# One level of Strassen's scheme for three adjacency products, with quarter sums kept in DRAM and layer 1 split into three runs of stages

## The chip, the cores and the metric

The kernel runs on one core of a Trainium2 chip. The metric is device time in microseconds (us), lower is better. Five engines take part, each with its own in-order stream of instructions: TensorE (PE in the profile, with its weight loads PEld), VectorE (DVE), ScalarE (ACT), GpSimd (POOL) and SyncE (SP). POOL, SP and ACT also issue DMA transfers. Whatever an engine has to wait for holds up everything behind it in its own stream.

## The reference

Two graph layers follow one another on x of shape (8, 2048, 64): 8 batches, 2048 nodes, 64 features. Everything is float32. Cut to what matters:

```python
# layer 0: supports I, A, 2AA - I     layer 1: supports I, A, 2AA - I, softmax(relu(E E^T))
w   = einsum('nd,dkio->nkio', embedding, weight)   # a weight matrix per node and support
x_g = einsum('knm,bmc->bnkc', supports, x)         # each support applied to x
out = einsum('bnki,nkio->bno', x_g, w) + embedding @ bias
x   = layernorm(x + out)
```

A is the 2048x2048 adjacency. With all batches side by side x is a 2048x512 matrix. Nobody forms AA: u = A x is computed first and then v = A u, so each layer has two products of the 2048x2048 matrix with a 2048x512 one. Layer 1 has a third one with the softmax matrix, s x.

## The kernel before

**Tiling.** Nodes are cut into 8 blocks of 256 (two slabs of 128 rows). A stage makes one block of one product. There are 32 stages in a row: stages 0 to 7 make u of layer 0, 8 to 15 make v of layer 0, 16 to 23 make u of layer 1, and 24 to 31 make v of layer 1 followed by z = s x for the same block. The adjacency streams in from DRAM through four tiles `a` of 512 KB, each holding four 128-row steps of the sum for a block, loaded by SP in the order of use (class `Ahead`). x and u stay in SBUF as 16 slabs of 128x512 each.

**Two ways to multiply.** For u, `product_u` holds a 128x128 piece of A still and moves a slab of x past it, 512 columns at a time: 32 matmuls a stage, output rows are nodes (`pu`). For v and z, `turned` holds a 128x128 piece of u or x still and moves 256 columns of A or of the softmax: 64 matmuls a stage and product, with features in the output's rows (`pv`). A float32 matmul leaves two records in the trace; the matmuls of `weights` use a faster number format and leave one.

**What rides beside a product.** The weights per node are made by `weights(g)`: two matmuls `pw` into a PSUM pair (`ps_big`, two pairs, shared by everything but the products) and one copy into `w_room`, by VectorE for even g and ScalarE for odd g; 16 g a stage, 8 for v of layer 0. `turn` transposes u or x so that features lie in the rows of `t` (8 transposes and 4 copies). `apply(c)` multiplies features with weights in small matmuls `po` and adds the result into `acc` on VectorE (operation SCALAR_TENSOR_TENSOR); four c a stage. `post` normalises the block on VectorE and ScalarE in three parts and stores it. In layer 0's v stages `scores_of_rows` and `statistics` also find the maximum and the sum of each softmax row: a maximum on VectorE, relu and exp on ScalarE, and then a reciprocal on VectorE that waits for the exp. The `scores` of z make the softmax tiles `p`.

**What sets the order.** The order is written by hand. Every job has a stage and a place from 0 to 64 within it (to 128 in the last eight stages), the function `put(n, place, f)`. The main loop runs the product of stage n, counts places (2 for a matmul of 512 columns, 1 for one of 256), and emits each job when its place is reached. `Pinned` keeps program order on each engine. Most of a stage's own finishing work (`weights`, `turn`, `apply`, `post`) is put into the following stage. In the last eight stages the weights share the stage's 128 places with two products.

**Ends.** A u stage ends with `end_u`, which copies PSUM into the slabs of `u_all`, one slab on VectorE and one on ScalarE. A v stage ends with `end_v`: in layer 0 this is put at place 6 of the next stage, and its result is needed by `apply` at place 20.

Of the kernel before, what the change touches and what calls it, by code (L numbers as in the profile page):

```python
# [8 lines left out]
F32 = mybir.dt.float32  # L9
# [5 lines left out]
P = 128  # L15
# [32 lines left out]
def two_graph_layers(ctx: ExitStack, tc: tile.TileContext, x, x_t, adj_b, layers, out):  # L48
# [30 lines left out]
    ps_acc = ctx.enter_context(tc.tile_pool(name="ps_acc", bufs=2, space=PSUM))  # L79
# [17 lines left out]
    X = [None] * NJ  # L97
# [3 lines left out]
    def new_x(j):  # L101
        X[j] = feat.tile([P, BC], F32, tag=f"x{j}", name=f"x{j}")
        return X[j]

    for j in range(NJ):
        act.dma_start(out=new_x(j), in_=x[j * P:(j + 1) * P, :])
# [75 lines left out]
    x1d = [dram.tile([NB * B, C], F32, tag=f"x1d{j}", name=f"x1d{j}") for j in range(NBLK)]  # L182
    cd = [dram.tile([2, SB, P], F32, tag=f"cd{j}", name=f"cd{j}") for j in range(NBLK)]
# [4 lines left out]
    def load_s1():  # L188
        for q in range(4):
            pool.dma_start(out=s1[q * D:(q + 1) * D, :].bitcast(F32), in_=estk[1][(q // 2) * D:(q // 2 + 1) * D, :])  # L190

    class Ahead:
# [6 lines left out]
        def next(self):  # L199
            while (len(self.ready) < self.bufs and self.order  # L200
# [6 lines left out]
    adj = Ahead(4, lambda: stream.tile([P, 4, NB], F32, tag="a", name="a"),  # L207
                lambda t, jm: sp.dma_start(out=t, in_=adj_b[jm[0]][:, jm[1]:jm[1] + 4, :]),
                [(j, m) for _ in range(4) for j in range(NBLK) for m in range(0, NJ, 4)])
# [5 lines left out]
    class Stage:  # L215
        def __init__(self, n, li, kk, j):
            self.n, self.li, self.kk, self.j = n, li, kk, j
            self.half = (li, kk) == (0, 1)
            self.units = C // 2 if self.half else C
            self.e01 = e01[n % 2]  # L220
            self.t = None


        def load_e(self):
# [5 lines left out]
            if (self.li, self.kk) == (1, 1):  # L230
                self.c = two.tile([P, 2, NB], F32, tag="c", name="c")
                pool.dma_start(out=self.c, in_=cd[self.j].rearrange("k s p -> k (s p)").partition_broadcast(P))
# [71 lines left out]
        def post(self, part, s0=0, s1=GROUPS):  # L304
# [20 lines left out]
            else:  # L325
# [10 lines left out]
                for s in range(s0 * SB // GROUPS, s1 * SB // GROUPS):  # L336
                    queue.dma_start(out=new_x(SB * self.j + s), in_=nodes[s * P:(s + 1) * P, :])


        def turn(self, k, slabs):  # L340
            ps = big("pt")
            psv = ps.rearrange("p a (q n) -> p (a q) n", n=P)
            for s in range(SB):
                for q in range(BQ):
                    pe.transpose(psv[:, s * BQ + q, :], slabs[SB * self.j + s][:, q * P:(q + 1) * P], ident)
            t = self.features()
            for s in range(SB):
                for par in range(2):
                    src = psv[64 * par:64 * par + 64, s * BQ:(s + 1) * BQ, :]
                    copy(s, t[64 * k:64 * k + 64, s * P:(s + 1) * P, par::2], src.rearrange("p q n -> p n q"))  # L350


        def graph(self):
            if self.kk == 0:
                return [(self.product_u(), self.end_u)]
            v = (self.turned(U, self.adjacency()), self.end_v)
            return [v] if self.li == 0 else [v, (self.turned(X, self.softmax()), self.end_z)]

        def adjacency(self):
            a = None  # L360
            for m in range(NJ):
                if m % 4 == 0:
                    a = adj.next()
                yield a[:, m % 4, :]
# [5 lines left out]
        def product_u(self):  # L370
            self.acc_u = ps_acc.tile([P, SB, BC], F32, tag="acc", name="pu")
            for m, a in enumerate(self.adjacency()):
                for s in range(SB):
                    pe.matmul(self.acc_u[:, s, :], a[:, s * P:(s + 1) * P], X[m],
                              start=(m == 0), stop=(m == NJ - 1))
                    yield 2

        def end_u(self):
            for s in range(SB):
                j = SB * self.j + s  # L380
                copy(s, U[j], self.acc_u[:, s, :])

        def turned(self, stationary, moving):


            self.acc_t = ps_acc.tile([P, BQ, NB], F32, tag="acc", name="pv")
            for m, a in enumerate(moving):
                for q in range(BQ):
                    pe.matmul(self.acc_t[:, q, :], stationary[m][:, q * P:(q + 1) * P], a,
                              start=(m == 0 and q % 2 == 0), stop=(m == NJ - 1 and q % 2 == 1))  # L390
                    yield 1

        def end_v(self):
            t = self.features()
            for h in range(2 if self.half else 1):
                for par in range(2):
                    src = self.acc_t[64 * par:64 * par + 64, :, :].rearrange("p q n -> p n q")
                    copy(1 - h, t[64 * h:64 * h + 64, :, par::2], src, 2.0)

        def end_z(self):  # L400
            t = self.features()
            for half in range(SB):
                n = slice(half * P, half * P + P)
                for par in range(2):
                    r = slice(64 * par, 64 * par + 64)
                    dve.tensor_tensor(t[64:128, n, par::2], self.acc_t[r, :, n].rearrange("p q n -> p n q"),
                                      self.c[r, 1, n, None].to_broadcast([64, P, BQ]), op=ALU.mult)
# [16 lines left out]
        def scores_of_rows(self, s, h):  # L424
# [9 lines left out]
            act.activation(w_room[:, (s + 4) * N + h * 1024:(s + 4) * N + (h + 1) * 1024], flat, AF.Relu)  # L434

        def statistics(self, s):
            j = SB * self.j + s
            r = w_room[:, (s + 4) * N:(s + 5) * N]
# [13 lines left out]


    later = [(0, 1, c) for c in range(V1 // 8)] + [(1, k, c) for k in range(2) for c in range(V0 // 8)]
    stages = [Stage(n, n // 16, n // 8 % 2, n % 8) for n in range(32)]
    stages[0].load_e()
    def units(x):
        return x.rearrange("p j x -> p (j x)").rearrange("p (v x) -> p v x", v=8)

    for c in range(V0 // 8):  # L460
        load_weights(0, 0, c, (units(u_all[:, 4 + 3 * c:6 + 3 * c, :]), units(u_all[:, 6 + 3 * c:7 + 3 * c, :])))
    split_rooms = [one.tile([P, 8, P], F32R, tag="wsplit", name="wsplit"),
                   one.tile([P, 8, P], F32R, tag="wraw", name="wsplit"),
                   units(u_all[:, 2:4, :]).bitcast(F32R),
                   one.tile([P, 8, P], F32R, tag="sq", name="wsplit")]
    for c in range(2):
        wst.ready.append(split_weights(0, 0, c, split_rooms[c]))
    wst.order = wst.order[2:]
    plans = [{} for _ in stages]

    def put(n, i, f, *args):
        plans[n].setdefault(i, []).append((f, args))

    def spread(n, first, last, jobs):
        for i, job in enumerate(jobs):
            put(n, first + (last - first) * i // max(len(jobs) - 1, 1), *job)

    for n, st in enumerate(stages):
        late = n < 24
        weights = [(st.weights, g) for g in range(st.units // 4)]  # L480
        if n == 15:
            spread(n, 44, 62, weights)
        elif st.half:
            spread(n + 1, 2, 16, weights)
        elif late:
            spread(n + 1, 1, 34, weights)
        else:
            spread(n, 52 if n == 24 else 28, 124, weights)
        if n + 1 < len(stages):
            if st.kk == 0:  # L490
                put(n + 1, 37, st.turn, 1, U)
            at, gap, posts = (8, 11, None) if n == 15 else (20, 14, 44) if st.half else (42, 9, 56) if late else (10, 9, 24)
            for c in range(4):
                put(n + 1, at + gap * (c // 2), st.apply, c)
            if n == 15:
                for k in range(6):
                    put(n + 1, (17 if k < 3 else 29) + k, st.post, k % 3, k // 3 * 8, k // 3 * 8 + 8)
            else:
                for k in range(3):
                    put(n + 1, posts + (3 if late else 4) * k, st.post, k)  # L500
# [96 lines left out]
```

## Time and profile before

| | before |
|---|---|
| median of 3 runs | 1678.39 us |
| lowest, highest of the 3 | 1666.79, 1689.35 us |
| the profiled execution | 1671.0 us |
| its span on the core | 1669.2 us |
| PE, PEld busy | 1609.2, 1117.6 us |
| DVE, ACT, POOL busy | 852.2, 469.0, 161.3 us |
| DMA moved | 206.38 MB, mean 124 GB/s |
| PE instructions | 10528 |

The span is the time from the first to the last instruction of one execution; the profiled execution's own time stands beside it. Busy times of the engines overlap one another. The profile also gives the clock granted to TensorE (PEclk, 1.00 is full speed); over the span its mean was 0.991.

The stages can be found in the trace by their ends (the copies `u<-pu` and `t<-pv`). Layer 0's u stages run from the start to 353.5 us, its v stages to 703.6 us, layer 1's u stages to 1061.4 us, and its v and z stages to 1649.5 us. The rest is the last block's finish.

### The profile page before, as it was taken

To read this page: it belongs to the slowest core of one execution; us is meant where nothing else is said; L and a number is where in the kernel's file an instruction comes from. 1 tells how busy PE (TensorE), PEld (TensorE's weight loads), DVE (VectorE), ACT (ScalarE), POOL (GpSimd) and SP (SyncE) were. 2 spreads that over 40 slices of the span, in tenths; PEclk is the share of its full clock that TensorE was granted. 3 is DMA by queue.
4 is the path that set the end of the run, shared out by engine and by line. 5 is a ranking of instruction groups with operands and counts; after the bars stand their busy time and mean duration, and the time that the engine had idled before them with its cause. 6 is when DMAs were issued, how large, how long until landed. Compare 5 with 4: busy or idle time off the path is not lost.

```text
span 1669.2 us, 24536 instructions
## 1 busy us (share of the span) xinstructions
PE 1609.2 (96%) x10528; PEld 1117.6 (67%) x10528; DVE 852.2 (51%) x1348; ACT 469.0 (28%) x518; POOL 161.3 (10%) x263
## 2 busy tenths in 40 slices
PE   8899999999899999899999999999999999999996
PEld 3455555567777777654555555778888888888885
DVE  3545555556676566664544444444353534425345
ACT  0122222222344444431222222231322314132231
POOL 4111111100111111110000000000000000000000
PEclk9999999999999999999999999999999999999998
DMA  9555665553545554445444444422231313223100
GB/s 353 180 167 171 188 192 175 187 164 120 144 133 137 112 116 118 110 100 136 128 142 142 130 141 137 141 85 73 89 98 48 101 60 95 66 77 98 51 26 13
DMA packets 63979, 206.38 MB, mean 124 GB/s; under 512 B 13056, under 2 KB 13056, under 8 KB 63296
## 3 DMA queue, kind: packets, MB, share of 16 engines
q1 hardware_dynamic: 38752, 126.37, 26.1%
q0 software_dynamic: 19648, 64.82, 13.3%
q10 hardware_dynamic: 5472, 13.63, 2.3%
q8 instruction: 83, 1.36, 0.3%
q14 instruction: 24, 0.20, 0.0%
HBM read 171.19 MB, written 33.57 MB: 123 GB/s over the span
## 4 chain that ended last, share of the span: by engine, by line
PE 53%; DVE 3%; issue 1%; DMA 1%; ACT 1%; SPq 0%; ACTq 0%
PE pv L42 26%; PE pu L42 11%; PE pw L42 7%; PE po L42 6%; DVE acc L42 1%; PE ps L42 1%; DMA wst<-wd 1%; PE pt L42 1%; DVE w L42 1%; ACT w L42 0%; ACT t L42 0%; DVE mean L42 0%; DVE dev L42 0%; DVE top L42 0%; DVE t L42 0%
## 5 line engine op out<-in xcount | busy, mean ns | idle before, releaser
L42 PE MATMUL pu<-x,a 128*128 128x512 f32 x1024 | 493.5, 600 | 5.8 <-DMA x<-in_x 5.8
L42 PE MATMUL pv<-a,u 128*128 128x256 f32 x2048 | 488.1, 384 | 7.4 <-issue 7.3
L42 DVE COPY w<-pw 128x1024 f32<-128x1024 f32 x224 | 273.8, 1224 | 323.2 <-PE pw L42 322.6
L42 PEld LDWEIGHTS pv<-a,u 128*128 128x128 f32 x2048 | 387.3, 191 | 75.9 <-issue 20.2
L42 PE MATMUL pw<-e,wst 128*128 128x512 f32 x880 | 394.9, 530 | 17.7 <-DMA wst<-wd 8.8
L42 ACT ACTIVATE w<-pw 128x1024 f32<-128x1024 f32 x224 | 229.1, 1023 | 421.8 <-PE pw L42 419.9
L42 DVE SCALAR_TENSOR_TENSOR acc<-po,mask,acc 128x256 f32<-128x256 f32 (+1 forms) x640 | 249.4, 427 | 179.6 <-PE po L42 157.4
L42 PEld LDWEIGHTS pu<-x,a 128*128 128x128 f32 x1024 | 190.1, 191 | 146.0 <-issue 120.7
L42 PEld LDWEIGHTS pw<-e,wst 128*128 128x128 f32 x880 | 164.3, 191 | 147.0 <-issue 94.1
L42 PE MATMUL pv<-p,x 128*128 128x256 f32 x1024 | 239.7, 379 | 0.0
L42 PE MATMUL po<-w,t 128*32 128x256 f32 (+1 forms) x5120 | 210.5, 338 | 6.1 <-issue 3.0
L42 PEld LDWEIGHTS pv<-p,x 128*128 128x128 f32 x1024 | 191.6, 190 | 26.6
L42 PEld LDWEIGHTS po<-w,t 128*32 128x32 f32 (+1 forms) x5120 | 124.8, 108 | 98.9 <-issue 39.8
L42 DVE SCALAR_TENSOR_TENSOR p<-ps,c 128x512 f32<-128x512 f32 x64 | 44.1, 689 | 92.9 <-PE ps L42 92.8
L42 ACT ACTIVATE p<-p 128x512 f32<-128x512 f32 x64 | 40.3, 630 | 117.3 <-DVE p L42 117.1
L42 ACT ACTIVATE sq<-acc 128x1024 f32<-128x1024 f32 (+2 forms) x20 | 17.7, 886 | 188.9 <-DVE acc L42 179.2
L42 ACT ACTIVATE w<-pr 128x1024 f32<-128x1024 f32 x32 | 32.7, 1023 | 116.2 <-DVE top L42 115.5
L42 ACT ACTIVATE u<-pu 128x512 f32<-128x512 f32 x16 | 9.6, 597 | 188.7 <-DVE u L42 188.7
L42 POOL DMA_DIRECT2D e<-ed x64 | 33.6, 530 | 288.8 <-PE pw L42 287.4
L42 DVE COPY t<-pt 64x512 f32<-64x512 f32 x48 | 33.1, 689 | 53.5 <-PE pt L42 50.4
L42 ACT ACTIVATE t<-pt 64x512 f32<-64x512 f32 x48 | 31.3, 651 | 103.3 <-DVE t L42 103.1
L42 ACT ACT_TABLE_LOAD x30 | 38.5, 1283 | 53.4 <-DVE p L42 27.4
(73 smaller groups left out, 632.0 us busy)
## 6 DMA issues: line engine op xcount, KB each, us to landing
a<-in_adj_b SPq DMA_DIRECT2D x128, 512.0 KB, 4.2
wst<-wd SPq DMA_DIRECT2D x110, 512.0 KB, 4.5
bx<-bx POOLq DMA_DIRECT2D x32, 256.0 KB, 3.0
acc<-bx POOLq DMA_DIRECT2D x16, 512.0 KB, 5.7
pd<-acc POOLq DMA_DIRECT2D x16, 512.0 KB, 2.9
acc<-pd POOLq DMA_DIRECT2D x16, 512.0 KB, 5.7
wd<-wsplit POOLq DMA_DIRECT2D x13, 512.0 KB
wraw<-in_w ACTq DMA_DIRECT2D x10, 512.0 KB, 7.9
```

Source lines behind the costliest of these rows:

```text
L42: return self._tc.keep_in_program_order(f(*args, **kwargs))
```

## The change

Stages are now named by a letter and a layer: A0 (u of layer 0), B0 (v of layer 0), A1 (u of layer 1), Z1 (z) and V1 (v of layer 1), eight each, 40 in all. Layer 1's v and z no longer share a stage: all of A1 comes first, then all of Z1, then all of V1; z goes to DRAM (`zd`) and comes back (`load_z`) for the V1 stage of its block.

**Strassen.** For B0, A1 and V1, blocks 1 to 7 are made from seven products of quarter size in place of eight (`strassen`). A block of A has 2x2 quarters (two slabs of rows, even and odd 128-column pieces); the right matrix has 2x2 quarters too (even and odd slabs, left and right 256 columns). Seven times eight matmuls of 256 columns are issued: 56 of the places, so `length` is 56 and every place is scaled by 56/64. VectorE forms the four results from the seven products with seven additions of 256 columns; ScalarE copies two of the products. Block 0 of each run stays `plain` (32 matmuls of 512 columns, all in the form that holds A still), and so do all of A0 and Z1.

**Sums of A.** While A0 reads the adjacency, `sums_of_a` makes the four sums of quarters on VectorE, four operations for each of the four `a` tiles of a stage, into one buffer `r`, which POOL stores in DRAM (`sd`). Later stages read three plain quarters and four sums: seven tiles of 512 KB a stage.

**Sums of the right matrix.** T1 to T4 are made once a phase by `Sums.make`, in operations of 2048 columns: during stage 8 (and the start of stage 9) for B0, during stage 16 for A1, and during stage 32 (and the start of 33) for V1. They lie in unused parts of `w_room`, in `u_all` and in `x_all`. As A1's sums overwrite u's place, A1's results go to a small tile `v` and to DRAM (`ud`), and SP reads them back in the Z1 stages.

**Turns.** As v now comes out with nodes in its rows, it must be transposed: `turn` runs for B0 and V1 also, at place 4 (B0) or 3 (V1) of the next stage. It is 8 transposes, with 8 copies in B0 and 4 in V1. `end_v` is gone. The accumulators in PSUM are four single banks in place of two pairs.

The core of the diff; `put(9, 0, ...)` is emitted before the first matmul of the stage:

```diff
-    ps_acc = ctx.enter_context(tc.tile_pool(name="ps_acc", bufs=2, space=PSUM))
+    ps_acc = ctx.enter_context(tc.tile_pool(name="ps_acc", bufs=4, space=PSUM))
...
+    plain = {("A0", j) for j in range(NBLK)} | {(phase, 0) for phase in ("B0", "A1", "V1")}
...
+    lefts = [("quarter", (0, 0)), ("quarter", (0, 1)), ("quarter", (1, 1)),
+             ("sum", 1), ("sum", 0), ("sum", 2), ("sum", 3)]
...
+        def turn(self, k, feature=None):
+            slabs = X[SB * self.j:SB * self.j + SB] if feature == "x" else self.slabs
+            scale = 2.0 if self.kk else None
...
             for s in range(SB):
-                for par in range(2):
-                    src = psv[64 * par:64 * par + 64, s * BQ:(s + 1) * BQ, :]
-                    copy(s, t[64 * k:64 * k + 64, s * P:(s + 1) * P, par::2], src.rearrange("p q n -> p n q"))
+                for h in range(2 if self.half else 1):
+                    for par in range(2):
+                        src = psv[64 * par:64 * par + 64, s * BQ:(s + 1) * BQ, :]
+                        copy(s, t[64 * (k + h):64 * (k + h) + 64, s * P:(s + 1) * P, par::2],
+                             src.rearrange("p q n -> p n q"), scale)
...
+        def strassen(self, right):
...
+            def times(name, what):
+                made[name] = acc = self.accumulator(name)[:, 0:half]
+                a = adj.next().rearrange("p (k n) -> p k n", n=P)
+                for k in range(k_slab):
+                    pe.matmul(acc, a[:, k, :], rights[what](k), start=(k == 0), stop=(k == k_slab - 1))
+                    yield 1
+            yield from times("p1", "B11")
+            act.copy(p1, made["p1"])
+            yield from times("p2", "B21")
+            add(c11, made["p2"], p1)
+            yield from times("p4", "T4")
+            act.copy(p4, made["p4"])
+            yield from times("p6", "T2")
+            add(u2, made["p6"], p1)
+            yield from times("p5", "T1")
+            add(u4, made["p5"], u2)
+            yield from times("p7", "T3")
+            add(c21, made["p7"], u2)
+            add(c22, made["p5"], c21)
+            add(c21, c21, p4, ALU.subtract)
+            yield from times("p3", "B22")
+            add(c12, made["p3"], u4)
+            self.store_u()
...
+        def sums_of_a(self, c):
+            q = self.a.rearrange("p (k t) (s n) -> p t s k n", t=2, s=2)
+            r = one.tile([P, 4, 2, P], F32, tag="sq", name="sums")
+            dve.tensor_tensor(r[:, 0], q[:, 0, 1], q[:, 1, 1], op=ALU.add)
+            dve.tensor_tensor(r[:, 1], r[:, 0], q[:, 0, 0], op=ALU.subtract)
+            dve.tensor_tensor(r[:, 2], q[:, 0, 0], q[:, 0, 1], op=ALU.subtract)
+            dve.tensor_tensor(r[:, 3], q[:, 1, 0], r[:, 1], op=ALU.subtract)
+            pool.dma_start(out=sd[self.j][:, :, 2 * c:2 * c + 2, :].rearrange("i p k n -> p i k n"), in_=r)
...
+        def make(self, i, k0=0, k1=NJ // 2):
+            cut = lambda a: a[:, k0:k1, :]
+            t, b11, b12, b21, b22 = ([cut(a) for a in self.t], *map(cut, (self.b11, self.b12, self.b21, self.b22)))
+            if i == 0:
+                dve.tensor_tensor(t[0], b12, b11, op=ALU.subtract)
+            elif i == 1:
+                dve.tensor_tensor(t[1], b22, t[0], op=ALU.subtract)
+            elif i == 2:
+                dve.tensor_tensor(t[2], b22, b12, op=ALU.subtract)
+            else:
+                dve.tensor_tensor(t[3], b22, t[0], op=ALU.subtract)
+                dve.tensor_tensor(t[3], t[3], b21, op=ALU.subtract)
...
+    put(0, 50, first_split, 0)
+    put(0, 60, first_split, 1)
...
+    for i, place in ((0, 54), (2, 57), (3, 60)):
+        put(8, place, sums["B0"].make, i)
+    put(9, 0, sums["B0"].make, 1)
+    for i in range(4):
+        put(16, 32 + 2 * i, sums["A1"].make, i, 0, 7)
+        put(16, 62, sums["A1"].make, i, 7, 8)
+    for i, place in ((0, 10), (2, 20), (3, 30)):
+        put(32, place, sums["V1"].make, i)
+    put(33, 0, sums["V1"].make, 1)
...
+        if phase == "A0":
+            for c in range(NJ // 4):
+                put(n, 16 * c + 10, st.sums_of_a, c)
             spread(n + 1, 1, 34, weights)
+            turned, bursts, posts = 37, (42, 51), (56,)
+        elif phase == "B0":
+            if st.j == 7:
+                spread(n, 44, 62, weights)
+                turned, bursts, posts = 2, (8, 19), ()
...
+            else:
+                spread(n + 1, 7, 19, weights)
+                turned, bursts, posts = 4, (22, 35), (44, 48, 52)
+            late = 12 if st.j == 7 else 0
+            for s, h, place in ((0, 0, 27), (0, 1, 30), (1, 0, 41), (1, 1, 44)):
+                put(n + 1, place + late, st.scores_of_rows, s, h)
+            for s, place in enumerate((32, 46)):
+                put(n + 1, place + late, st.statistics, s)
+        elif phase == "A1":
+            spread(n + 1, 7, 36, weights)
+            turned, bursts, posts = 4, (42, 51), (56,)
+        elif phase == "V1":
+            spread(n, 28 if st.j else 4, 62, weights)
+            turned, bursts, posts = 3, (9, 18), (26, 30, 34)
+            put(n, 20, st.load_z)
```

## The prediction

> **What bounds the kernel now.** I read the busy shares first, then the chain that ended last, then busy time by stretch.
>
> ```profile
> PE 1609.2 (96%) x10528; PEld 1117.6 (67%) x10528; DVE 852.2 (51%) x1348; ACT 469.0 (28%) x518; POOL 161.3 (10%) x263
> ...
> PE 53%; DVE 3%; issue 1%; DMA 1%; ACT 1%; SPq 0%; ACTq 0%
> ```
>
> TensorE is busy 96% of the span, and of the chain's engines it alone is long. So fewer matmuls are worth their time, wherever VectorE keeps up. The view by stretch (length, busy us of PE, PEld, DVE, ACT, POOL, then PEclk) says where it does; rows are stages 2 to 7, 9 to 14, 15, 16, 17 to 23, and 25 to 31:
>
> ```profile
> 88.40:353.50 265.10, 264.40 (x1412) 137.86 (x1410) 144.91 (x197) 60.58 (x66) 31.23 (x51) 1.00 0.56 172
> ...
> 394.90:652.20 257.30, 238.76 (x2451) 195.51 (x2450) 167.61 (x344) 108.20 (x107) 32.51 (x51) 0.97 0.51 127
> 652.20:703.60 51.40, 44.14 (x427) 34.78 (x426) 32.69 (x62) 21.88 (x23) 7.02 (x10) 1.00 0.56 128
> 703.60:743.20 39.60, 37.31 (x346) 19.26 (x344) 26.11 (x64) 15.04 (x18) 7.99 (x13) 1.00 0.44 129
> 743.20:1061.40 318.20, 314.13 (x1694) 166.28 (x1693) 153.88 (x218) 79.89 (x92) 28.61 (x45) 0.99 0.46 131
> ...
> 1144.80:1649.50 504.70, 503.12 (x3035) 421.08 (x3037) 214.12 (x294) 132.42 (x154) 20.26 (x29) 1.00 0.23 71
> ```
>
> Layer 1 is all TensorE. Layer 0's v stages are not: 257.3 us for six, 18.5 of it idle, the clock at 0.97. There VectorE and ScalarE hand work to each other in a row. From the timeline of stage 9:
>
> ```profile
> 413.60 1.21 DVE L42 TENSOR_REDUCE top<-pr 128x1 f32<-128x1024 f32 x1
> ...
> 419.76 0.17 DVE L42 RECIPROCAL inv<-total 128x1 f32<-128x1 f32 x1 [2.65 <-ACT w L42]
> 419.84 4.21 DVE L42 SCALAR_TENSOR_TENSOR acc<-po,mask,acc 128x128 f32<-128x128 f32 x16
> ...
> 432.01 0.16 DVE L42 RECIPROCAL inv<-total 128x1 f32<-128x1 f32 x1 [2.67 <-ACT w L42]
> ...
> 433.95 1.23 DVE L42 TENSOR_TENSOR acc<-acc,rstd 128x1024 f32<-128x1024 f32 x1
> ```
>
> VectorE stands twice behind an exp on ScalarE. The first `po` burst began at 408.24, the normalising multiply ended at 435.1: 26.9 us in a row, of a 38.5 us stage (`t<-pv` at 399.08 and 437.56). Before, nothing that TensorE needs soon is queued behind it.
>
> **What is removed.** Thirty records of 256 columns start at 389.53 and the next instruction at 395.92: 0.213 us a record, 0.427 a matmul. Seven products for eight save 8 matmuls, 3.41 us, in 21 stages: **-71.7 us**. Weight loads stay hidden: v already loads new weights for every 256 columns at this pace. 8 transposes take 0.87 us (they start at 1039.97, the next matmul at 1040.84); 16 more turns cost **+13.9 us**. Were TensorE the bound throughout, the 1671.0 us of the profiled execution would become 1613. The rest of the sum is what each run of stages keeps of this.
>
> **A1, -23.9.** Stages 17 to 23 turned u before. VectorE is busy 153.88 of 318.20 us; seven additions of 0.43 us (the 128x256 subtraction of `mean` took 425 ns) add 3 us to a stage of 41.5. After the last `po` burst 4.9 us of product remain, enough for its additions before the turn. All is kept (-18 if the closer-packed weights stall).
>
> **Z1 and V1, -10** (-17 to -3): -23.9 and +7.0 for eight turns. V1 puts `post` (5.3 us of VectorE) at places 26 to 34, across weights that start at 28; two PSUM pairs hide about a microsecond less than needed: +5 for seven stages. V1's sums: T4's two operations take 4.6 us by the slope of the rows 512 columns 0.691 and 1024 columns 1.225 us, and weight copies come to VectorE every 4.2 us: +3 with T2. About 1 us less is spent on switching matmul kinds.
>
> **A0, +8** (0 to 20). Four sums of 0.43 us and their dependent starts make 1.9 us per tile, 7.6 us a stage. VectorE had 144.91 busy of 265.10 us, so there is room; at place 26 they run into `bias` (place 28) and the weight copies, about 1 us a stage. The next sums wait for `r` to be stored: from places 58 to 10 there are some 7 us for a store whose nearest rows are 2.9 (`pd<-acc`) and 9.3 us (`t<-in_x_t`); I take the middle, no wait, and the upper bound from the second. The weight splits moved into stage 0 may make the first weights later: +2 (0 to 4).
>
> **Entry to B0, +8.5.** T1, T3 and T4 are four operations of 2.29 us (the slope again), 9.2 in all, put in front of the copy of v's slab. The last burst's additions end 6.0 us after it starts (`po` near 298.85, VectorE until 304.85), so the slab is copied at 6.0+9.2+0.7+0.2 = 16.1; TensorE reaches the turn at 3.6+6x0.853+4x0.427 = 10.4. Gap 5.7 us, 1.2 more as T2 holds the turn's copies, and a slow clock after it (below). Queued behind the turn on TensorE is everything.
>
> **Entry to A1, +11.5.** Five operations of 1792 columns, 10.1 us, go in before the first row maximum. The turn of x, at 731.07 before, needs that maximum's PSUM pair: VectorE finished `post` at 727.5, so 727.5+10.1+1.2+1.0 (relu) makes 740, a 9 us gap; the late chain then costs the next turn 1 more, and the clock 1.7. Both entries lie between 5 and 15 us.
>
> **B0's steady stages, +16** (-18 to +34). Now the turn at place 4 needs the last result of `strassen`, and the order of the built program has these additions on VectorE behind that row of maxima, exps and `post`. The row: 26.9 us in stage 9, 28.4 in stage 11 (495.01 to 523.40), plus two additions and one ScalarE copy inside it, three additions behind it, the last one, and hand-over: 3.1. That is 30 to 31.5 us from first burst to turn. From turn to first burst TensorE needs 0.87 + 16x0.427 + 16x0.213 + 0.4 of switching + 1.0, as the turn's eight copies (2.8 us on VectorE) hold a PSUM pair: 12.5. Together 42.5 to 44, where TensorE's own work would be 36.5. So each stage gets a gap of 3 to 4 us at the turn. The waits that the trace calls "issue" and "remote" (4.67, 2.0, 2.94, 2.7 us in four of the six stages) lie in `po` and its additions, which stay: +2. Half clock after the gap: +0.7. I take 45.6 against 42.9 before, +2.7 in six stages and nothing in stage 15. The saving of 3.41 is eaten.
>
> **The clock** is what a gap costs on top.
>
> ```profile
> 586.48 1.19 PE L42 MATMUL pr<-s,es 128*128 128x512 f32 x2 [2.94 <-DVE acc L42]
> ...
> 586.50:590.00 3.50, 3.50 (x8) 2.79 (x9) 2.64 (x5) 2.05 (x2) 0.00 (x0) 0.50 0.13 50
> ```
>
> After 2.94 us without matmuls the granted clock is 0.50 for the next stretch, and 0.65 until 593.5; after 1.9 us it was 0.50 once (626.60 to 630.00) and 1.00 once (695.50 to 699.00). One slow period costs 1.7 to 3.4 us of work, less where TensorE waits anyway. The Trainium skill ("TensorE: Matmul & The Clock Gate", Part 1) says that the clock halves after at least one idle window of about 3.4 us. By that rule most of B0's gaps would stay just under the limit and B0 would cost some 5 us less; the rows gate sooner, and the rows decide.
>
> **The sum.** -23.9 - 10 + 8 + 2 + 8.5 + 11.5 + 16 = +12, so 1683 on the profiled execution's 1671.0. The median of the runs, 1678.39, is 1.0044 times that: **1690 us**. Two per cent, 33.6 us, is about what a measurement of this kernel can tell from no change, as its runs spread from 1666.79 to 1689.35.
>
> **Rivals.**
> *The gain is kept in B0.* VectorE is busy only 167.61 of 257.30 us there; if its chain ends before the fourth matmul of the next stage, B0 gives -18 for +16 and the entries cost half: 12-34-10-8 = -40, or 1638. Against it stands the order of the additions. 0.13.
> *Every gap in B0 halves the clock in full.* There are two places per stage: the turn, and the second pair of row maxima, where `pr` waited 1.2 us and longer before. From 2.9 us a gap is certain to count; then seven stages lose 3.4 us more each, and 12+24 = +36 makes 1714, slower. The idle time at 0.97 clock speaks for it. 0.20.
> *The one buffer of A0's sums.* A store that lands after 9 us stops VectorE and then TensorE for 2.5 us more a stage: +20, 1710; with the case before, 1734. POOL's large stores landed within 5.2 us, against it. 0.12.
> *That fewer products aren't issued* is excluded: the built order has 1176 matmuls of 256 columns for the three products and 352 of 512.
>
> **Chances.** The forecast, no change beyond 2%, has 0.55. Faster than 1645: 0.13, the first rival. Slower than 1712: 0.32, the second and third. The range runs from 1648, between forecast and first rival, to 1730, where the two slow rivals meet; some 2 in 10 lie outside.
>
> **What would show it.** Right: PE's busy time about 60 us lower while the span stays; new waits of the transposes `pt` on VectorE in B0; a granted clock below 0.97 there; A1 stages of 41.5 us and Z1 plus V1 of about 70.5. Wrong: B0 stages near 38 us, or weight matmuls in A0 waiting for the sums. What would upset the sum most is VectorE being later, or sooner, at the turn than this count has it.

## The result, and the profile after

| | before | after |
|---|---|---|
| median | 1682.05 us | 1740.79 us |
| lowest, highest of 4 runs | 1666.79, 1689.35 us | 1737.89, 1743.24 us |
| span of the profiled execution | 1669.2 us | 1741.5 us |
| mean granted clock | 0.991 | 0.971 |
| PE, DVE busy | 1609.2, 852.2 us | 1584.2, 995.8 us |

The changed kernel takes 1.0361 times as long, 95% interval 1.0283 to 1.0438. It is slower, by 3.6 per cent, and lies above the range that was given (1648 to 1730 us).

The page of the kernel after, busy shares and the chain that ended last:

```profile
PE 1584.2 (91%) x10640; PEld 1140.5 (65%) x10640; DVE 995.8 (57%) x1670; ACT 457.5 (26%) x557; POOL 211.3 (12%) x343
...
PE 63%; DVE 20%; issue 7%; ACT 4%; DMA 4%; POOL 1%; another core or an unknown queue 0%; DVEq 0%; ACTq 0%; POOLq 0%
```

TensorE is busy 25 us less, and the span is 72 us longer. Busy time times mean clock is 1538 us against 1595, an estimate from this table: 56 us less work at full clock, near the 58 that the prediction took off on TensorE (71.7 less 13.9). VectorE's part of the chain rose from 3 to 20 per cent, "issue" from 1 to 7. So the matmuls went, and waits came. The view by stretch of the kernel after (length, busy us of PE, PEld, DVE, ACT, POOL, then PEclk, DMA share, GB/s) says where. The rows are stage 1, stages 2 to 7, stages 9 to 15 with their entry, stage 16, ten microseconds at the start of stage 17, stage 17, stages 18 to 23, and Z1 with V1:

```profile
35.20:101.60 66.40, 48.98 (x238) 24.46 (x237) 46.68 (x73) 10.12 (x12) 15.91 (x24) 0.87 0.67 218
101.60:391.60 290.00, 270.72 (x1405) 138.50 (x1404) 175.59 (x287) 60.66 (x67) 48.85 (x74) 0.98 0.63 201
...
435.50:780.40 344.90, 283.82 (x2842) 226.78 (x2847) 222.15 (x468) 137.34 (x159) 40.44 (x62) 0.94 0.56 137
780.40:829.60 49.20, 36.09 (x337) 19.06 (x337) 35.18 (x71) 15.63 (x20) 4.83 (x7) 0.90 0.40 83
...
825.00:830.00 5.00, 2.86 (x14) 1.96 (x13) 2.61 (x7) 2.21 (x3) 0.98 (x2) 1.00 1.05 28
830.00:835.00 5.00, 4.36 (x24) 3.52 (x22) 2.60 (x3) 1.93 (x3) 0.85 (x2) 1.00 0.85 34
...
829.60:884.20 54.60, 44.11 (x291) 34.47 (x292) 23.91 (x37) 11.41 (x14) 5.81 (x10) 0.91 0.65 147
884.20:1142.30 258.10, 249.77 (x1746) 197.31 (x1745) 146.30 (x226) 69.69 (x87) 29.73 (x49) 1.00 0.60 187
1142.30:1717.30 575.00, 568.60 (x3365) 458.56 (x3364) 299.81 (x417) 136.25 (x179) 44.58 (x75) 1.00 0.42 129
```

In layer 1's last rows TensorE is busy 97 to 99 per cent, as it was. Before that there is idle time in every row, 19 us of it in stages 2 to 7, which had less than one. Set beside the same stretches of the kernel before (ends taken here where TensorE goes from one stage's product to the next; the rows above end at the copies `u<-pu`, `t<-pv`, `v<-pu`, `t<-pt`, up to 5 us later):

| stretch | before | after | difference | forecast |
|---|---|---|---|---|
| stage 1 | 53.4 | 66.4 | +13.0 | +2 |
| stages 2 to 7 | 265.1 | 290.0 | +24.9 | +8 |
| stage 8 | 41.4 | 43.9 | +2.5 | 0 |
| stages 9 to 15 with the entry | 308.7 | 340.2 | +31.5 | +24.5 |
| stage 16 | 38.8 | 50.0 | +11.2 | +11.5 |
| A1, stages 17 to 23 | 318.0 | 315.9 | -2.1 | -23.9 |
| Z1 and V1 | 586.2 | 575.9 | -10.3 | -10 |
| tail | 22.5 | 24.2 | +1.7 | 0 |

The sum is +72.4 against a forecast of +12, and two places hold most of the 60 us between: layer 0's u stages (28) and A1 (22). What made stage 8 and the tail longer was not looked into. The timeline of the kernel after, one sum of `sums_of_a` and what followed, a turn in B0, the entry to A1, and stage 17:

```profile
245.17 0.76 POOL L42 DMA_DIRECT2D sd<-sums  x1 [0.49 <-DVE sums L42]
...
254.04 0.43 DVE L42 TENSOR_TENSOR sums<-a 128x256 f32<-128x256 f32 x1 [3.11 <-DMA sd<-sums]
...
265.90 1.22 PE L42 MATMUL pw<-e,wst 128*128 128x512 f32 x2 [3.03 <-DVE w L42]
...
485.41 0.88 PE L42 MATMUL pt<-ident,v 128*128 128x128 f32 x6 [2.98 <-DVE v L42]
...
814.18 1.97 PE L42 MATMUL pt<-ident,x 128*128 128x128 f32 x8 [8.99 <-ACT w L42]
...
849.67 0.42 DVE L42 TENSOR_TENSOR v<-p,temps 128x256 f32<-128x256 f32 x1 [10.64 <-DMA ud<-v]
...
851.28 1.22 PE L42 MATMUL pw<-e,wst 128*128 128x512 f32 x2 [9.10 <-DVE w L42]
```

Five readings. The sums wait for the store of the sums before them: issued at 245.17, it lets VectorE on at 254.0, 8.8 us later; behind VectorE stand copies of weights, and TensorE waits for those. The turn in B0 waits 3 us for the last addition. The turn of x waits 9 us, as forecast, behind sums of x. In stage 17 an addition into `v` waits 10.6 us for the store of block 0's u, issued at 829.74, and TensorE stands for 9.1 us. And in the ten microseconds around the issue of that store (825 to 835) the DMA engines are busy nearly all the time (share 1.05 and 0.85) and move 28 to 34 GB/s, where stages 2 to 7 have 201 GB/s at a share of 0.63. The two small stores of the statistics of block 7 were issued just before, at 824.24 and 827.22.

### The profile page after: what moved, and what is told of

It reads as the page before. It is cut to its first block, busy times and chain, and to the rows that moved or that the text cites. A ratio compares the mean times of both kernels' runs of the same rounds, so it can differ in the third digit from the quotient of the medians.

```text
span 1741.5 us, 25540 instructions
## 1 busy us (share of the span) xinstructions
PE 1584.2 (91%) x10640; PEld 1140.5 (65%) x10640; DVE 995.8 (57%) x1670; ACT 457.5 (26%) x557; POOL 211.3 (12%) x343
## 4 chain that ended last, share of the span: by engine, by line
PE 63%; DVE 20%; issue 7%; ACT 4%; DMA 4%; POOL 1%; another core or an unknown queue 0%; DVEq 0%; ACTq 0%; POOLq 0%
PE p L42 20%; PE pz L42 12%; PE pw L42 10%; PE po L42 9%; PE pu L42 9%; DVE acc L42 8%; DVE w L42 3%; ACT w L42 3%; DMA sd<-sums 2%; PE pt L42 2%; DVE top L42 2%; DVE mean L42 1%; DVE t L42 1%; DMA ud<-v 1%; DVE sums L42 1%
## 5 line engine op out<-in xcount | busy, mean ns | idle before, releaser
L42 PE MATMUL p<-u,a 128*128 128x256 f32 x1344 | 348.4, 391 | 0.0
L42 PEld LDWEIGHTS p<-u,a 128*128 128x128 f32 x1344 | 258.8, 196 | 52.7 <-issue 11.0
L42 PE MATMUL pu<-x,a 128*128 128x512 f32 x576 | 282.0, 613 | 5.5 <-DMA x<-in_x 5.5
L42 PE MATMUL pz<-p,x 128*128 128x256 f32 x1024 | 234.2, 379 | 0.0
L42 PEld LDWEIGHTS pz<-p,x 128*128 128x128 f32 x1024 | 189.9, 190 | 24.6 <-issue 0.8
L42 PEld LDWEIGHTS pu<-x,a 128*128 128x128 f32 x576 | 109.4, 195 | 92.1 <-issue 74.8
L42 PE MATMUL p<-x,a 128*128 128x256 f32 x672 | 166.4, 380 | 0.0
L42 PEld LDWEIGHTS p<-x,a 128*128 128x128 f32 x672 | 126.0, 189 | 23.4 <-issue 3.4
L42 DVE SCALAR_TENSOR_TENSOR p<-ps,c 128x512 f32<-128x512 f32 x64 | 44.2, 691 | 115.8 <-PE ps L42 115.4
L42 PE MATMUL p<-w,a 128*128 128x256 f32 x336 | 84.9, 395 | 1.8 <-issue 1.8
L42 PEld LDWEIGHTS p<-w,a 128*128 128x128 f32 x336 | 65.5, 197 | 14.1 <-issue 4.0
L42 POOL DMA_DIRECT2D e<-ed x80 | 42.1, 531 | 168.1 <-PE pw L42 136.3
```

Source lines behind the costliest of these rows:

```text
L42: return self._tc.keep_in_program_order(f(*args, **kwargs))
```

## The experiments

Each run's ratio is to runs of the kernel before on the same chip (medians 1694.22 us for the first four runs, 1683.8 for the next four, 1684.25 for the combined ones, 1679.18 and 1678.63 for the last three). Times of stretches come from one profiled execution of a run. How far they scatter shows in B0, which two of the runs leave as it is: from its first turn to its last it took 333.4 us in the kernel after, 336.2 in the run with two buffers for the sums, and 338.4 in the run with a changed stage 0.

### One buffer for the sums of A

```diff
-            r = one.tile([P, 4, 2, P], F32, tag="sq", name="sums")
+            if c % 2:
+                whole = one.tile([P, 4, 2, P], F32, tag="sq", name="sums")
+                r = [whole[:, i] for i in range(4)]
+            else:
+                pair = [two.tile([P, 2, NB], F32, tag="c", name="sums").rearrange("p i (k n) -> p i k n", n=P)
+                        for _ in range(2)]
+                r = [pair[i // 2][:, i % 2] for i in range(4)]
```

Even c use the two tiles `c`, which are idle until Z1, and store each by itself.

> The sums of A alternate between two buffers: the old one for the second and fourth tile of a stage, two idle 2 KB tiles for the first and third. Nothing else changes. Theory 1 (the single buffer r is what A0 pays for: VectorE waits for the store of the sums before and TensorE then waits for VectorE's weight copies): VectorE's waits for the store, 28.4 us in the changed kernel, fall below 5; the A0 stages 2 to 7 fall from 48.3 us to about 45 (-20), stage 1 from 66.4 to about 60; the kernel becomes 20 to 28 us faster than the changed one, 1713 to 1721 us. Theory 2 (it is VectorE's work and the stores' traffic as such): stages 2 to 7 stay within 1 us of 48.3 and the kernel within 6 us of 1741.

Measured: 1717.51 us, ratio 1.0169 (1.0107 to 1.0232). Stages 2 to 7 by stretch:

```profile
93.48:359.87 266.39, 264.74 (x1405) 136.65 (x1404) 175.41 (x287) 60.60 (x67) 57.22 (x86) 1.00 0.68 219
```

The stretch is 266.4 us, 23.6 less, TensorE has 1.6 us idle and the clock is whole; stage 1 fell by 9 as well. The same additions (VectorE 175.41 us busy against 175.59) now cost 1.3 us beside the kernel before. So it was the one buffer, and not VectorE's work.

### Reciprocals, B0 plain, and a later turn

Three edits on B0. First, the two reciprocals that wait for an exp leave their places for place 62:

```diff
-            dve.reciprocal(inv[:, j:j + 1], total)
+            self.totals.append((j, total))
...
+            put(n + 1, 62, st.invert)     # the two reciprocals
```

> The two reciprocals of a B0 block, each of which holds VectorE until an exp on ScalarE has ended, are moved to place 62, behind the last part of the normalisation and the additions of the seventh product; all else stays. Theory 1 (B0 is bound by the row of VectorE and ScalarE work from the first burst to the turn): the row gets shorter by the two waits, 2.7 to 4 us and 2.3 us; the transposes' wait for v on VectorE, 17.1 us in stages 10 to 16, goes below 5, and the B0 stages fall from 42.2 to 52.5 us by 4 to 5 each: the kernel becomes 25 to 35 us faster than 1741. Theory 2 (the long B0 stages come from TensorE waiting for its instructions and from the half clock after that): less than 10 us faster.

Measured: 1728.49 us, ratio 1.0225 (1.0163 to 1.0287). The seven turns take 318.4 us, 15 less; the transposes still wait 21.5 us for v in the whole run (24.4 in the kernel after). The first theory had that wait below 5. Two of the five microseconds that the reciprocals held in a stage came back: in the normalisation VectorE now waits 2.4 us for `dev` from ScalarE, where the kernel after has 0.4, in each of the six steady stages. VectorE's stand behind the exps is a part of the row, no more.

Second, no Strassen in B0, and no sums of u:

```diff
-    plain = {("A0", j) for j in range(NBLK)} | {(phase, 0) for phase in ("B0", "A1", "V1")}
+    plain = {("A0", j) for j in range(NBLK)} | {(phase, 0) for phase in ("A1", "V1")} | {("B0", j) for j in range(NBLK)}
```

> All eight B0 blocks are made in the plain form (32 matmuls of 512 columns), with no sums of u; the turn and all places in 64ths stay, A1 and V1 keep Strassen, and the sums of A are still made. Theory 1 (B0's row of VectorE and ScalarE work, not TensorE, sets its stages): giving up 7 x 3.41 = 23.9 us of TensorE's saving costs nothing or gains, since the additions leave the row: B0 stages of 41 to 47 us, the entry's gap of 4.85 us goes, the kernel is 5 to 30 us faster than 1741. Theory 2 (Strassen's saving is partly kept in B0): it is 10 to 24 us slower, 1751 to 1765.

Measured: 1734.45 us, ratio 1.0258 (1.0197 to 1.0319). The turns take 323.5 us, 10 less, though B0 issues 8 matmuls a stage more; the wait for v falls to 6.7 us. In B0 Strassen's 24 us are eaten and some more.

Third, weights first and then the turn, nothing taken away:

```diff
-                spread(n + 1, 7, 19, weights)
-                turned, bursts, posts = 4, (22, 35), (44, 48, 52)
+                spread(n + 1, 1, 13, weights)
+                turned, bursts, posts = 16, (22, 35), (44, 48, 52)
```

> The changed kernel with the order in B0's stages 9 to 15 turned round: weights at places 1 to 13, then the turn at 16, the bursts at 22 and 35 as before. No work is taken away. Theory 1, B0 is bounded by the row on VectorE from first burst to turn plus TensorE's way from turn to burst (42 to 44 us): with the weights out of that way the wait of the transposes for v goes from 22.0 us to under 4, the turns from 447 to 780 take 290 to 310 us in place of 333.4, ratio about 1.02. Theory 2, VectorE is merely late everywhere: the gap moves to the bursts or to the weights, the seven turns take 325 us or more, ratio 1.033 to 1.04.

Measured: 1738.84 us, ratio 1.0333 (1.0287 to 1.0379). The wait for v is gone, but `po` waits 9 us for the turn's copies, `pw` 19 us for its own, and from the end of stage 8 to that of stage 16 only 7 us are gained. (The seven turns take 316.8 us, but they begin later in the stage here and end as before, so I go by the stages.) In the time, the second theory holds.

### The small stores of the statistics

First the stores of `cd` were moved to another queue:

```diff
-                pool.dma_start(out=cd[self.j][k].rearrange("s p -> p s"),
+                act.dma_start(out=cd[self.j][k].rearrange("s p -> p s"),
```

> The stores of the softmax statistics, element by element, go through ScalarE's queue in place of POOL's; nothing else changes. Theory 1 (A1's first Strassen stage waits because the store of its predecessor's result stands behind these stores in POOL's queue): VectorE's wait of 10.6 us for that store and TensorE's 9.1 us go away, stage 17 falls from 54.6 to about 44 us, the kernel becomes 8 to 12 us faster than 1741, 1729 to 1733. Theory 2 (the store of v is slow by itself, about 19 us): the wait stays and the time is within 3 us of 1741.

Measured: 1730.21 us, ratio 1.0227 (1.0155 to 1.03). Stage 17 takes 56.2 us, where the kernel after has 54.6; by that my theory fell. B0's turns took 317.3 us, 16 less, which I had not expected. So the stores were made once instead:

```diff
+    def store_c():                        # stage 20, place 40
+        for k, a in enumerate((cst, inv)):
+            pe.transpose(ps[0:NJ, k, 0:P], a, ident)
+        dve.tensor_copy(c, ps[0:NJ, :, 0:P])
+        pool.dma_start(out=cd.rearrange("k j p -> j k p"), in_=c)
...
-            put(n + 1, 62, st.store_c)
```

> The changed kernel with the statistics of the softmax stored once, transposed on TensorE into 32 rows of 512 bytes in stage 20, in place of 16 stores of 256 elements of 4 bytes at the end of B0's stages. Theory 1, the 4-byte stores hold the DMA engines for some 10 us each time, and what comes behind them is late (the store of u in stage 17, and the fetches behind TensorE's waits called issue): stage 17 falls from 56.2 to 45 to 47 us, the issue waits of TensorE between the first and last turn of B0 from 13.4 us to under 5, together -15 to -22 us, ratio about 1.025. Theory 2, the store of u is late by the loads of weights and sums queued beside it: stage 17 stays at 54 to 57 us, -6 us or less.

Measured: 1717.42 us, ratio 1.0191 (1.0143 to 1.0239). The waits of TensorE (us in all, times, longest) from the first turn of B0 through stage 17, in the kernel after:

```profile
PE pt L42 <- DVE v L42: 24.1, 8, 4.8
PE pw L42 <- DVE w L42: 18.7, 10, 9.1
...
PE po L42 <- issue: 6.7, 3, 5.3
PE pr L42 <- issue: 4.9, 1, 4.9
```

The same in this kernel:

```profile
PE pt L42 <- DVE v L42: 23.4, 8, 4.8
...
PE pw L42 <- DVE w L42: 12.6, 9, 2.0
...
PE po L42 <- issue: 0.3, 1, 0.3
```

And its stage 17 by stretch:

```profile
819.80:863.20 43.40, 42.66 (x295) 34.08 (x294) 23.99 (x37) 11.30 (x14) 4.98 (x8) 0.99 0.56 166
```

Both effects are there: stage 17 takes 43.4 us, 11.2 less (the longest store of u lands after 9.3 us, not 19.2), and the issue waits are gone. B0's turns take 317.3 us. With the stores on ScalarE's queue the issue waits fell too, from 13.4 to 2.0 us, but u's store stayed late, so these are two effects of the same stores. The issue waits may be late fetches of instructions (the profile's page lists DMA queues of kind instruction, q8 with 84 packets), but no run shows it. The Trainium skill ("DMA: Bandwidth & Descriptors", "Rules for kernel authors") says that a last dimension with a stride becomes one descriptor per element, and ("Issuing engines are not separate DMA queues") that DMAs issued by ScalarE, SyncE or GpSimd run on the same 16 DMA engines. The stores were 256 elements of 4 bytes each. On ScalarE's queue the sixteen of them add 4352 packets, 272 each, which agrees with the first; on GpSimd's they make only 512, so there the trace doesn't show it. That stage 17 was not shorter with the other queue, with u's store landing after 19.9 us in place of 19.2, agrees with the second.

The same edit on the kernel before:

> The kernel before with the statistics stored once, as in the run before last of this call. Theory 1, the 4-byte stores cost the kernel before something as well: its issue waits in stages 9 to 15 (pv 7.3, po 3.0 us) fall below 4 us, ratio 0.993 to 0.996. Theory 2, they cost only where u is stored in stage 17: ratio 0.998 to 1.001.

Measured: 1654.28 us, ratio 0.982 (0.978 to 0.986), more than either theory had. The issue waits of `pv` and `po` in stages 9 to 15 fell from 10.3 to 3.8 us. So these stores hurt both kernels, and the loss by the change itself is not explained by them: 1717.42 against 1654.28 is again 1.038.

### Stage 0

`plain` holds block 0 of every phase, so nobody reads the sums that stage 0 makes.

```diff
-            for c in range(NJ // 4):
+            for c in range(NJ // 4 if n else 0):
                 put(n, 16 * c + 10, st.sums_of_a, c)
...
-    put(0, 50, first_split, 0)
-    put(0, 60, first_split, 1)
+    put(0, 0, first_split, 0)
+    put(0, 0, first_split, 1)
```

> The changed kernel without the 16 additions and 4 stores of stage 0 (no stage reads the sums of block 0, as the first stage of each phase is plain), and with the first two weight splits back ahead of stage 0's product. Theory 1, those additions and the late splits are what makes stage 1 13 us longer (66.4 against 53.4 us): stage 1 takes 53 to 56 us, the span falls by 10 to 13 us from 1741.5, ratio to before about 1.029. Theory 2, stage 1 is long because its own sums and its stores crowd VectorE and POOL's queue: stage 1 stays at 60 us or more, span -6 us or less.

Measured: 1737.47 us, ratio 1.0326 (1.0277 to 1.0374). Stage 1 takes 47.7 us, 18.7 less, better than before's 53.4; the span fell by 8.9 only, as B0's turns took 5 us more (issue waits of 19.5 us here, 13.4 there) and stage 16 took 2.6 more. Theory 1 holds for the stage. The run changed the sums and the splits together; two buffers alone, with both still in place, gave 9 of the 18.7 us.

### All together

The four mended places in one kernel, then with the later turn:

> Four edits together: no sums and early splits in stage 0, two buffers for the sums, both reciprocals at place 62, statistics stored once. Theory 1, each answers for another stretch, so their gains add: stage 1 -17 to -18, stages 2 to 7 -23, B0's turns 333 to 300 us or less, stage 17 -12, in all 1655 to 1670 us of span, ratio to the kernel before 0.985 to 1.00. Theory 2, they fill the same gaps, as VectorE stays late in B0 and at both entries whatever is moved: 1685 us or more, B0's turns 312 us or more.

> The run before this one with weights first and the turn at place 16 in B0. Theory 1, once the fetches and the reciprocals are out of the way, what is left of B0's gaps is the row from first burst to turn, and the order breaks it: the turns take 265 to 280 us for seven stages, 15 to 25 us below the run before this one. Theory 2, VectorE's work between the bursts (row maxima, additions) makes the gaps wherever the turn stands: within 6 us of the run before this one.

Measured: 1648.16 us, ratio 0.9795 (0.9752 to 0.9838), and 1638.9 us, ratio 0.9737 (0.9684 to 0.9789). The waits of TensorE in B0 with the four edits:

```profile
PE pt L42 <- DVE v L42: 20.6, 7, 4.8
PE pw L42 <- DVE w L42: 7.9, 9, 1.0
```

And with the later turn as well:

```profile
PE pw L42 <- DVE w L42: 12.1, 9, 4.9
PE po L42 <- ACT t L42: 11.9, 8, 1.5
...
PE pt L42 <- DVE v L42: 0.2, 1, 0.2
```

The gains add, to more than expected: 94 us of span for the four edits, where the four runs alone gave 78. A stage of B0 takes 40.8 us with the four edits, though the turn still waits nearly as long as in the kernel after (2.6 to 2.7 us). The later turn removes that wait and puts as much into shorter ones; what it brings is 1.4 us a stage (39.4), with the granted clock at 1.00 in place of 0.96 over the six stages. That lies between the theories, nearer the second.

Then A1's places, and A1's sums on GpSimd:

```diff
-            spread(n + 1, 7, 36, weights)
+            spread(n + 1, 9, 37, weights)
...
-        put(16, 32 + 2 * i, sums["A1"].make, i, 0, 7)
+        put(16, 14 + 2 * i, sums["A1"].make, i, 0, 7, pool)
```

> The run before this one with A1's weights at places 9 to 37 in place of 7 to 36, and the first seven eighths of A1's sums on GpSimd from place 14 of stage 16. Theory 1, A1 lost its gain to the turn's copies on ScalarE that hold a PSUM pair (0.64 us a stage) and the bias on VectorE (0.74 us), and entry A1's 9 us to the sums on VectorE: A1's stages fall from 42.97 to 41.6 to 42.3 us, stage 16 from 50 to 43 us or less, 10 to 17 us in all. Theory 2, the waits move with the weights, and GpSimd's sums are so slow (or slow VectorE so much) that stage 17 waits for them: 5 us or less in all.

Measured: 1635.23 us, ratio 0.9716 (0.9672 to 0.9759), 7.4 us less of span, between the theories. A1's stages take 42.1 us. The stretch from the last turn of B0's blocks to the end of stage 16 only went from 43.9 to 42.8: the 7.5 us wait of the turn of x is gone, but `pb` now waits 5.7 us for "issue"; why stays open.

And B0 plain in this kernel, with the turn at place 4:

> The first of these four with A1's places and GpSimd's sums as in the run before this one, and B0 plain: no Strassen there, turn at place 4. Theory 1, B0's row on VectorE takes away what Strassen saves there even with all else mended: this is within 8 us of the run before this one, or faster. Theory 2, with the row broken by the later turn Strassen's 24 us in B0 are real: this is 12 to 24 us slower than the run before this one.

Measured: 1635.33 us, ratio 0.9723 (0.968 to 0.9766), the same. B0's stages take 41.1 us, 1.7 more each, and its entry is shorter, as sums and additions go. Even mended, Strassen in B0 is worth nothing beside this. B0 plain with the later turn was not run.

### What the scheme and the order are worth

> The kernel before with the two edits that mend it as well: statistics stored once, reciprocals at place 62. Theory 1, the change itself costs time only where it was laid out badly, and what the mended versions gained over the kernel before is half due to these two: 1640 to 1655 us, ratio 0.975 to 0.982, that is 0.3 to 1 per cent slower than the best version. Theory 2, the two edits explain all of it, and Strassen adds nothing: 1635 us or less, ratio 0.972 or below.

For the second, no block is made by Strassen:

```diff
+    plain = {(phase, j) for phase in ("A0", "B0", "A1", "V1") for j in range(NBLK)}
...
-                put(n, 16 * c + 10, st.sums_of_a, c)
```

> The last of the four combined versions with no Strassen at all: A1 and V1 plain too, no sums of A in A0 and none of x or u. Its turns and its order stay. Theory 1, seven products for eight are worth what was counted: 7 x 3.41 us in A1 and in V1 less some 5 us for sums and additions, so this is 35 to 50 us slower than the version with Strassen in A1 and V1 (1668 to 1683 us, ratio 0.992 to 1.00). Theory 2, additions and hand-overs eat half of it there too: 10 to 25 us slower.

Measured: the kernel before with its two edits 1633.1 us, ratio 0.9719 (0.9704 to 0.9733), as fast as the versions of the change so far. That is the second theory's time, but not for its reason, that Strassen adds nothing: without Strassen the change takes 1663.48 us, ratio 0.9894 (0.9876 to 0.9911), 28 us slower than with it in A1 and V1, between the theories. Five stages of A1 without it by stretch, and a part of A1 with it:

```profile
778.26:1004.30 226.04, 225.45 (x1213) 118.07 (x1212) 110.41 (x156) 56.83 (x65) 25.50 (x41) 1.00 0.45 142
...
783.80:1025.00 241.20, 237.58 (x1651) 186.62 (x1653) 137.60 (x210) 68.16 (x84) 29.44 (x47) 1.00 0.63 193
```

TensorE is all but always busy in both. An A1 stage takes 45.2 us against 42.1, a V1 stage 43.3 against 41.0: 3.1 and 2.3 of the 3.41 us counted arrive. A0 as a whole is as long with the sums of A as without (317.1 and 317.5 us). So the scheme pays some 30 us in layer 1, and the new order with its 16 turns costs 30.

That suggests a version that beats all: B0 as in the kernel before (`turned`, no turns), Strassen in A1 and V1, the rest mended.

```diff
+            if self.half:
+                return self.turned_v()    # the old product and end_v, on two single banks
...
-                turned, bursts, posts = 4, (22, 35), (44, 48, 52)
+                turned, bursts, posts = None, (20, 34), (44, 47, 50)
+                put(n + 1, 6, st.end_v)
```

> The last of the four combined versions (Strassen in A1 and V1, the rest mended) with B0 as in the kernel before: the product comes out turned and there is no turn. From the other traces, B0's stages take 38.0 to 39.0 us in the mended kernel before and 41.05 us in that version, A1's 42.1 against 44.9, one stage of z and one of v together 70.6 against 73.5. Theory 1, the turns alone make B0 dear, and the stretches add: B0 -14 to -20 us, so 1613 to 1622 us, ratio 0.96 to 0.966, better than the mended kernel before (0.972) by the scheme's worth in A1 and V1. Theory 2, B0's shorter stages leave the sums and entry A1 less room, so that 5 us or less remain: 1630 us, ratio 0.969 or above.

Measured: 1617.72 us, ratio 0.9626 (0.9565 to 0.9686). By stretch, six stages of B0 in this kernel:

```profile
401.90:631.40 229.50, 227.22 (x2449) 191.77 (x2448) 162.15 (x348) 110.66 (x120) 23.08 (x36) 1.00 0.39 124
```

And in the kernel before with its two edits:

```profile
398.40:630.50 232.10, 228.37 (x2450) 191.89 (x2449) 169.13 (x345) 108.24 (x108) 25.23 (x40) 1.00 0.44 142
```

These are 38.3 and 38.7 us a stage, where the plain form with a turn took 41.1. The span is 17.1 us below that version's, as theory 1 had it; so B0's form with its turns makes 17 of the 30 us that the new order costs. It is the fastest of all, 3.7 per cent below the kernel before and one per cent below the mended kernel before.

## Why the prediction was wrong

**Z1 and V1** (-10, measured -10.3; in V1 TensorE waits 5.1 us for weight copies of VectorE, where 5 stood), the **entry to A1** (+11.5, measured +11.2, with the 9 us wait in its place) and the **gap of the entry to B0** (5.7 forecast, 4.85 us found) were right. Right too was the mechanism in **B0**: a gap at every turn, 2.98 us in the one shown where 3 to 4 stood, and Strassen's saving eaten. Its size was off by 1.2 us a stage: 46.8 on average over the six steady stages, not 45.6. Without the small stores they take 44.2 us (317.3 in all seven turns). There the row from the first `po` to the turn takes 28.4 to 30.6 us, where 30 to 31.5 stood, and the way from the turn to the next `po` 13.8 to 15.3, where 12.5 stood: the way is the term that was too small, by some 2 us. The small stores add 2.6 us a stage, where I took +2 for the issue waits (of the four waits behind that figure, the two called issue stood before `pv`, not in `po`). With the four edits row and way still make the stage. From the timeline of TensorE in that kernel:

```profile
461.95 2.03 PE L42 MATMUL po<-w,t 64*32 64x128 f32 x128
...
488.52 1.18 PE L42 MATMUL pt<-ident,v 128*128 128x128 f32 x6 [2.63 <-DVE v L42]
...
502.76 2.03 PE L42 MATMUL po<-w,t 64*32 64x128 f32 x128
```

That is 26.6 us and 14.2 us, together the 40.8 us of a stage, within 0.3 us alike in all six: a shorter row, and the turn still waits for its end.

**A0** is where the forecast failed first. The step was "a store whose nearest rows are 2.9 and 9.3 us; I take the middle, no wait". The stores did land after 5.6 us at the median, yet in the case shown VectorE was let on 8.8 us after the issue, where 512 KB stores of weights and of `pd` stood ahead in POOL's queue (issued 243.61 and 244.15), and it waited 28.4 us in all. In those 8.8 us the DMA engines were also full (share 1.00, 353 GB/s, loads issued by SP among them); whether the queue or the traffic made the store late, no run separates. The third rival had this mechanism, at +20 beyond the +8; stages 2 to 7 came out 16.9 us beyond, and I gave it 0.12. Against it I had set that large stores landed within 5.2 us, but 5.2 is the median of the slowest kind (`x1d<-acc`), not a limit. And with two buffers stages 2 to 7 are only 1.3 us longer than before, so of the +8 for VectorE's work little came there. When the next use stands 7 us off and the rows around span 3 to 9, no wait is not the middle.

**The start** (+2, measured +13): the step was "the weight splits moved into stage 0 may make the first weights later". They stood behind sums that wait for stores (these begin 5.4 and 5.9 us after the issue of the store before), and TensorE waited 10.5 us for the first split; the run without those sums, and with the splits put back, gave 18.7 us back. That these sums are read by nobody stands in the diff, and I had not seen it.

**A1** (-23.9, measured -2.1): the step was "all is kept". Three things took 21 us: 11.2 in stage 17, where v is overwritten while its store is behind the small ones; 0.64 us a stage where the second `pw` waits for the turn's copies on ScalarE to free a PSUM pair; and 0.74 us a stage behind the bias on VectorE. Weights two places later, and the sums on GpSimd, took the second away and left 0.6 of the third (42.1 us a stage). I had counted VectorE's time there, and neither the pairs nor the one buffer `v`.

**The clock.** After the 3.03 us gap the clock was 0.57 in the next 3.4 us (266.0 to 269.4) and then 1.00. After the 2.98 us gap in B0 it was 1.00 at first (485.5 to 488.9) and 0.77 in the 3.4 us after that, in which TensorE was busy only 1.87 us, so the gap and this idle time are not told apart. So a gap of about 3 us can be followed by half the clock, as in the rows of the kernel before; the rule of an idle window of about 3.4 us, which the prediction weighed (the Trainium skill, "TensorE: Matmul & The Clock Gate", Part 1), does not hold for the first of these by the profile's times. B0 as a whole had 0.94, so a part of the second rival happened as well.

## What to carry to other kernels

A store from a single buffer is a wait on VectorE's path: price it at its landing among the other transfers of that moment, for every use, and ask who stands behind the waiting engine. When a change takes work from TensorE, list every shared buffer that the freed time would now run into, PSUM pairs too, and look for work whose result nobody reads. And mend the faults that both versions share before a change is judged: two small edits made the old kernel as fast as the first mended new ones, and only then did it show which half of the change was worth keeping.

## What the hardware showed that I had not expected

Sixteen stores of 1 KB, in pieces of 4 bytes, cost the kernel before 1.8 per cent (ratio 0.982). Its spread went too, as far as few runs tell: on one chip its seven runs lie between 1675.0 and 1693.1 us and the four without these stores between 1649.6 and 1656.0; on another the seven lie between 1675.7 and 1683.4 and the four with both edits between 1632.2 and 1633.9. GpSimd adds 128x1792 elements in 4.0 to 4.4 us by the profile, where VectorE takes 2.0.
